# A two-layer decoder on one core: the first attention's scores from fp32r pairs in row tiles, wider query chunks, and PSUM in slots of two banks

## The chip, the cores and the metric

The kernel runs on one core of one Trainium2 chip. The metric is the device time of one execution in microseconds, from start to end on that core. TensorE multiplies matrices into PSUM (eight banks of 2 KiB per partition), VectorE and ScalarE read PSUM, GpSimd works on SBUF alone, and the DMA transfers are issued from the SyncE queue (SP).

## The reference

The input is `x`, 4 batches of 1024 tokens with 256 channels in fp32, and a context of 77 tokens a batch. Six blocks follow each other, each on a layer norm of `x` and added back to it: a causal attention with 16 heads of 16 dimensions and a linear bias by distance; a cross attention; a feed-forward block with quantized weights; then a second causal attention with squared scores and gates; a cross attention; and a feed-forward block with 4-bit quantization. The change is about the first of them:

```python
att = einsum('bhqd,bhkd->bhqk', q, k) / sqrt(16)
att = att + where(causal, slope[h] * (k_pos - q_pos), -inf)
y   = einsum('bhqk,bhkd->bhqd', softmax(att), v)
x   = x + y @ w_proj.T
```

and, through its use of PSUM, about the second attention too:

```python
P = where(causal, (q.k)**2 * exp(log_G[q] - log_G[k]), 0)   # scaled by its row's maximum
y = (P @ v) / sum(P)
```

## The kernel before, in words

The program is written as Python generators that are woven into each other by counts, and a scheduler of the framework then sets the final order on each engine when the program is built. That order is fixed at run time: each engine runs its instructions in it, and waits on semaphores.

The first attention of batch b (`A0`) runs together with a side stream: the preparation of weights for b = 0, and for later batches the cross attention and feed-forward block of batch b-1 (`XA`, `F0`). Towards the end of `A0` the front of the next batch (`qkv`, the first stacks, the first maxima) is woven in. Then comes the second attention (`A1`) with the blocks of the batch before as its side stream, and at the end the last feed-forward block in four lanes.

The first attention works in groups of four heads, 16 groups in all (4 batches of 4).

- `qkv` makes q and k transposed, splits each into three bf16 parts (L288 to L291, on ScalarE, VectorE and GpSimd) and stores them to DRAM (L294, L295). `stacks` loads them back as QS and KS, 96 rows in which the parts meet each other, and 12 to 14 rows more for the bias (L317 to L320). A product over these 108 or 110 rows gives a score near fp32.
- `a0_max` makes scores with queries on the partitions (tile M, L346), masks the diagonal with a matmul of the identity with a mask (L350), and takes row maxima on VectorE (L351). `a0_put_max` transposes the maxima and writes them as two more rows into QS (L377).
- `a0_main` makes the scores again with keys on the partitions (tile S, L392), in query chunks of 256, two heads to a bank. It masks (L394), ScalarE takes the exponential into P (L395), and after a lag of two units PV multiplies by V, which has a column of ones for the sum (L404). PV is plain fp32; its four heads go to four column tiles of 32.
- `o_out` transposes and divides (L418 to L425), `proj_res` projects and adds (L438 to L450).

PSUM tiles are one bank. `BANKS` gives each use its banks, taken in turn: in the first attention S has banks 0 and 1, M and Q banks 2 and 3, U bank 0; T and W of the side stream have 4, 5 and 6, and O has 7. In the second attention S, Q, U and D share 0 to 3. There, `scores` makes a unit of four heads in two banks (L867), takes absolute values of each bank on VectorE (L873) or ScalarE (L871), squares them (L875) and on the diagonal multiplies by a decay (L878); `decay` makes two banks with one exponential each (L841, L842).

Helpers record much under one line: L189 is every matmul of `mm3` (three fp32r products for one near fp32), and L177 and L178 are the split of an fp32 tile into a high and a low part.

Of the kernel before, what the change touches and what calls it, by code (L numbers as in the profile page):

```python
# [24 lines left out]
H = 16  # L25
D = 16
NEG = -30000.0
ABS_ACT = (1, 5)


def const_arrays():
# [6 lines left out]
    c["maskb"] = np.where(k > q, NEG, 0.0).astype(bf)  # L38
    c["maskTb"] = np.ascontiguousarray(c["maskb"].T)
# [22 lines left out]
    parts = []  # L62
    r = sl.astype(np.float64)
    for _ in range(3):
        p = r.astype(bf)
        parts.append(p)
        r = r - p.astype(np.float64)
    pos = np.arange(T)
    hi = (pos // 8 * 8).astype(np.float64)
    lo = (pos % 8).astype(np.float64)  # L70
    rq = np.zeros((H, 12, T), np.float64)
    rk = np.zeros((H, 14, T), np.float64)
    for h in range(H):
        r = 0
        for p in parts:
            s = float(p[h])
            for w in (hi, lo):
                rq[h, r], rk[h, r] = s, w
                rq[h, r + 1], rk[h, r + 1] = w, -s
                r += 2  # L80
        rk[h, 12:] = 1.0
    c["alq"] = np.ascontiguousarray(rq.transpose(1, 0, 2)).astype(bf)
    c["alk"] = np.ascontiguousarray(rk.transpose(1, 0, 2)).astype(bf)
# [3 lines left out]
NF0, NP0, NS0 = 10, 8, 30  # L87
# [3 lines left out]
class Kern:  # L91
    MAGIC = 12582912.0
    LAG0, LAG1 = 2, 2
    GQ, NQ = (2, 2, 2, 2), (12, 12, 12, 12)
    NW = ((25, 25, 38, 38),) * 4

    def const(self, *names):
        for nm, dt in names:
            t = self.cp.tile([96 if nm == "ind" else 128, 128], dt, name=nm)
            self.nc.sync.dma_start(t, self.c[nm])  # L100
            setattr(self, nm, t)
# [3 lines left out]
    def __init__(self, ctx, tc, ins, out, consts, nb=B):  # L105
# [23 lines left out]
    BANKS = (  # L129
        {"S": (0, 1), "M": (2, 3), "M0": (0, 1, 2, 3), "Q": (2, 3), "U": (0,), "D": (0, 1), "O": (7,), "T": (4, 5, 6), "W": (4, 5, 6)},  # L130
        {"S": (0, 1, 2, 3), "Q": (0, 1, 2, 3), "U": (0, 1, 2, 3), "D": (0, 1, 2, 3), "O": (7,), "T": (4, 5, 6), "W": (4, 5, 6), "TB": (0, 1, 2, 3), "WB": (0, 1, 2, 3)},
    )
# [19 lines left out]

    def p(self, tag):
        self.n += 1
        banks = self.BANKS[self.phase][tag]
        self.turn[banks] = self.turn.get(banks, -1) + 1
        k = banks[self.turn[banks] % len(banks)]
        return self.ps.tile([128, 512], F32, tag=f"B{k}", name=f"{tag}_{self.n}", bufs=1)
# [68 lines left out]
    def xT(self, xn, h, l, tag="T"):  # L227

        n = xn.shape[1]
        for c in range(2):  # L230
            ps = self.p(tag)
            for j in range(n):
                self.nc.tensor.transpose(ps[:, j * 128 : (j + 1) * 128], xn[:, j, c * 128 : (c + 1) * 128], self.ident)
            self.evac_hl(h[:, c, :], l[:, c, :], ps[:, : n * 128])
# [27 lines left out]
    def qkv(self, src, wd, nw, gl=None, w=None):  # L262
# [4 lines left out]
        for c in range(2):  # L267
            self.n += 1
            dr.append(self.dr.tile([8, 128, T], BF, tag=f"dr{c}", name=f"dr{c}_{self.n}", bufs=2))
        for half in range(2):  # L270
# [10 lines left out]
            for c in range(2):  # L281
                pt = self.t([128, 6, 512], BF, "qp")
                for s in range(2):
                    ps = self.p("Q")
                    o = s * 256 + c * 128
                    self.mm3(ps, [(wh[:, k, o : o + 128], wl[:, k, o : o + 128]) for k in range(2)], [(h[:, k, :], l[:, k, :]) for k in range(2)])
                    r = self.t([128, 512], F32, "qr")
                    nc.scalar.activation(pt[:, 5 * s], ps, AF.Copy)  # L288
                    nc.vector.tensor_tensor(r, ps, pt[:, 5 * s], ALU.subtract)
                    nc.gpsimd.tensor_scalar(pt[:, 1 + 3 * s], r, 1.0, 1.0, ALU.mult, ALU.mult)  # L290
                    nc.gpsimd.tensor_tensor(pt[:, 2 + s], r, pt[:, 1 + 3 * s], ALU.subtract)  # L291
                    yield
                d = dr[c]
                nc.sync.dma_start(d[1:7, :, hs].rearrange("t p n -> p t n"), pt)  # L294
                nc.sync.dma_start(d[0::7, :, hs].rearrange("t p n -> p t n"), pt[:, 0::5])  # L295
            n = 256 if gl is None else 272
            for e in range(4):
                ps = self.p("Q")
                i = half * 4 + e
                tk = slice(e * 128, (e + 1) * 128)  # L300
                self.mm3(ps[:, :n], [(h[:, k, tk], l[:, k, tk]) for k in range(2)], [(wh[:, k, 512 : 512 + n], wl[:, k, 512 : 512 + n]) for k in range(2)])
                nc.scalar.activation(vv[half][:, e, :, 0:16], ps[:, :256].rearrange("p (h e) -> p h e", h=H), AF.Copy)
                if gl is not None:
                    nc.scalar.activation(gl[:, i, :], ps[:, 256:272], AF.Copy)
# [3 lines left out]
    def stacks(self, g, dr, alibi):  # L308

        nc = self.nc  # L310
        QS = self.t([110, 4, T], BF, "QS")
        KS = self.t([110, 4, T], BF, "KS")
# [5 lines left out]
        if alibi:  # L318
            nc.sync.dma_start(QS[96:108], self.c["alq"][:, g * 4 : g * 4 + 4, :])
            nc.sync.dma_start(KS[96:110], self.c["alk"][:, g * 4 : g * 4 + 4, :])  # L320
# [3 lines left out]
    def prep_a0(self):  # L324
        self.wa0 = self.prep_w(self.i["L0_attn_w_attn"], 768, "wa0", 256)
        self.const(("identb", BF), ("maskb", BF), ("maskTb", BF))
# [6 lines left out]
    def a0_max(self, st, mt, tag="M"):  # L333
# [4 lines left out]
        def unit(pieces, diag, out):  # L338

            S = self.p(tag)  # L340
            n = len(pieces)
            w = pieces[0][3] - pieces[0][2]
            st_ = 512 // n
            Sv = S.rearrange("p (n k) -> p n k", n=n)
            for x, (hh, i, k0, k1) in enumerate(pieces):
                nc.tensor.matmul(Sv[:, x, 0:w], QS[:108, hh, i * 128 : (i + 1) * 128], KS[:108, hh, k0:k1], start=x == 0, stop=not diag and x == n - 1)  # L346
            if diag:
                r = self.maskb if n == 1 else self.maskb.unsqueeze(1).to_broadcast([128, n, 128])
                o = Sv[:, 0, w - 128 : w] if n == 1 else Sv[:, :, w - 128 : w]
                nc.tensor.matmul(o, self.identb, r, start=False, stop=True)  # L350
            nc.vector.tensor_reduce(out, Sv[:, :, 0:w], AX.X, ALU.max)  # L351

        for part in range(2):
            b0 = part * 4
            yield unit([(hh, b0, part * 512, part * 512 + 128) for hh in range(4)], True, mt[:, :, b0])
            for p in range(2):
                yield unit([(p * 2 + e, b0 + 1, part * 512, part * 512 + 256) for e in range(2)], True, mt[:, p * 2 : p * 2 + 2, b0 + 1])
            for i in (2, 3):
                for hh in range(4):
                    yield unit([(hh, b0 + i, part * 512, part * 512 + (i + 1) * 128)], True, mt[:, hh, b0 + i : b0 + i + 1])  # L360
        for i in range(4, 8):
            for hh in range(4):
# [906 lines left out]
```

## Time and profile before

| what | value |
|---|---|
| median of 3 runs | 2571.21 us (2570.82 to 2571.67) |
| profiled execution | 2593.41 us, its span 2591.4 us, granted TensorE clock 0.914 |
| TensorE matmul busy | 2214.7 us |
| VectorE busy | 1769.4 us |
| ScalarE busy | 1592.7 us |
| GpSimd busy | 1227.5 us |
| DMA, mean | 96 GB/s |
| first S to last S of the first attention (L392) | 137.6 to 1354.2 us |
| first S to last S of the second attention (L867) | 1371.9 to 2438.0 us |

A row of a group of instructions has the line, the engine and the operation, the tile written and those read, the shapes, the count, the busy time with the mean of one in ns, and the engine's idle time before them with what ended it. For matmuls the shape has rows and columns of the array in front ("110*128"). A plain fp32 matmul leaves two records in the trace, so L404 counts 2560 where the program has 1280. A row of a stretch has for each engine its busy time and count, then the granted TensorE clock, the DMA share and GB/s. A row of the timeline has the start in us, the time until the last of its instructions ends, and how many are merged. A row of waits has the total, the number of times, and the longest.

### The profile page before, as it was taken

To read this page: it belongs to the slowest core of one execution; us is meant where nothing else is said; L and a number is where in the kernel's file an instruction comes from. 1 tells how busy PE (TensorE), PEld (TensorE's weight loads), DVE (VectorE), ACT (ScalarE), POOL (GpSimd) and SP (SyncE) were. 2 spreads that over 40 slices of the span, in tenths; PEclk is the share of its full clock that TensorE was granted. 3 is DMA by queue.
4 is the path that set the end of the run, shared out by engine and by line. 5 is a ranking of instruction groups with operands and counts; after the bars stand their busy time and mean duration, and the time that the engine had idled before them with its cause. 6 is when DMAs were issued, how large, how long until landed. Compare 5 with 4: busy or idle time off the path is not lost.

```text
span 2591.4 us, 51361 instructions
## 1 busy us (share of the span) xinstructions
PE 2214.7 (85%) x19057; PEld 1575.9 (61%) x19094; DVE 1769.4 (68%) x3865; ACT 1592.7 (61%) x4099; POOL 1227.5 (47%) x2026
## 2 busy tenths in 40 slices
PE   5698889988989999899887997798879887879887
PEld 4455446754556755566545774476667666757676
DVE  3556555667566577566777677678857886677787
ACT  3255435666656676556666996786658674867532
POOL 6121302144321242213446467657875677565665
PEclk9689889999999999999997998898989998979888
DMA  8856540223652225122262211521162215333000
GB/s 228 184 133 178 163 103 13 68 62 108 158 146 58 67 81 183 41 68 55 73 189 80 73 53 64 168 83 47 64 167 72 57 65 165 86 111 83 10 9 17
DMA packets 170287, 248.44 MB, mean 96 GB/s; under 512 B 13734, under 2 KB 146166, under 8 KB 161430
## 3 DMA queue, kind: packets, MB, share of 16 engines
q1 hardware_dynamic: 170038, 245.17, 34.9%
q8 instruction: 150, 2.46, 0.4%
q14 instruction: 99, 0.81, 0.1%
HBM read 162.65 MB, written 82.21 MB: 94 GB/s over the span
## 4 chain that ended last, share of the span: by engine, by line
PE 50%; DVE 17%; DMA 13%; POOL 7%; ACT 5%; issue 3%; SPq 1%; POOLq 0%; ACTq 0%; DVEq 0%
PE T L189 8%; PE W L189 7%; PE O L404 6%; PE Q L189 4%; PE M L346 4%; PE S L392 4%; PE O L895 4%; PE S L867 3%; DMA KS<-c_alk 2%; DVE P L873 2%; DMA MD<-R 2%; DVE s_mt L351 2%; DMA UD<-R 1%; DMA QS<-dr 1%; PE T L716 1%
## 5 line engine op out<-in xcount | busy, mean ns | idle before, releaser
L351 DVE TENSOR_REDUCE s_mt<-M 128x1 f32<-128x512 f32 (+3 forms) x608 | 386.4, 656 | 161.7 <-PE M L350 112.8
L395 ACT ACTIVATE P<-S 128x512 f32<-128x512 f32 (+1 forms) x640 | 342.0, 564 | 167.5 <-PE S L392 87.1
L875 ACT ACTIVATE P<-P,eps 128x1024 f32<-128x1024 f32 (+1 forms) x320 | 341.6, 1091 | 68.5 <-DVE P L873 66.0
L873 DVE TENSOR_REDUCE P<-S 128x512 f32<-128x512 f32 (+1 forms) x480 | 281.4, 609 | 62.9 <-PE S L867 55.5
L189 PE MATMUL T<-R,xX 128*128 128x308 f32 (+1 forms) x1328 | 303.6, 340 | 13.2 <-DMA R<-g1d 3.1
L346 PE MATMUL M<-KS,QS 108*128 108x512 bf16 (+3 forms) x768 | 229.5, 347 | 54.7 <-DVE s_mt L351 21.3
L616 POOL TENSOR_TENSOR E<-E,s_xsm 128x616 f32<-128x616 f32 x88 | 108.3, 1231 | 323.5 <-DVE s_xsm L614 209.3
L392 PE MATMUL S<-QS,KS 110*128 110x256 bf16 (+1 forms) x1280 | 232.0, 270 | 27.9 <-ACT P L395 14.3
L613 ACT ACTIVATE E<-T,s_xmx 128x77 f32<-128x77 f32 x704 | 223.9, 361 | 41.4 <-DVE s_xmx L610 35.5
L189 PEld LDWEIGHTS T<-R,xX 128*128 128x128 f32 x1328 | 221.3, 197 | 42.4 <-ACT E L613 8.7
L189 PE MATMUL W<-R,xph 128*128 128x256 f32 (+2 forms) x1192 | 241.2, 299 | 4.3 <-DVE xpl L178 3.3
L867 PE MATMUL S<-QS,KS 96*128 96x256 bf16 (+1 forms) x1280 | 213.3, 273 | 35.1 <-DVE P L873 24.8
L404 PE MATMUL O<-P,V 128*32 128x256 f32 (+1 forms) x2560 | 241.4, 376 | 0.0
L189 PEld LDWEIGHTS W<-R,xph 128*128 128x128 f32 (+2 forms) x1192 | 195.0, 200 | 17.0 <-DVE xpl L178 4.9
L878 POOL TENSOR_TENSOR P<-P,y 128x512 f32<-128x512 f32 x128 | 168.2, 1320 | 68.0 <-ACT P L875 40.5
L189 PE MATMUL W<-R,xpl 128*128 128x256 f32 (+2 forms) x596 | 178.4, 299 | 3.3 <-DVE xpl L178 3.2
L392 PEld LDWEIGHTS <-KS 110*128 110x128 bf16 x1280 | 105.2, 100 | 110.2 <-issue 54.2
L867 PEld LDWEIGHTS <-KS 96*128 96x128 bf16 x1280 | 104.1, 100 | 102.3 <-issue 73.4
L613 ACT ACTIVATION_READ_ACCUMULATOR E<-T,s_xmx 128x1 f32 x704 | 166.1, 242 | 0.0
L177 ACT ACTIVATE xph<-W 104x128 fp32r<-104x128 f32 (+1 forms) x228 | 102.4, 475 | 97.1 <-PE W L627 35.3
L895 PE MATMUL O<-P,VsJ 128*32 128x128 f32 x3584 | 157.0, 282 | 5.3 <-ACT P L875 3.5
L346 PEld LDWEIGHTS <-QS 108*128 108x128 bf16 x768 | 69.4, 102 | 131.7 <-issue 103.2
(357 smaller groups left out, 5493.3 us busy)
## 6 DMA issues: line engine op xcount, KB each, us to landing
QS<-dr SPq DMA_DIRECT2D x72, 384.0 KB
KS<-dr SPq DMA_DIRECT2D x72, 384.0 KB
dr<-qp SPq DMA_DIRECT2D x32, 768.0 KB
MD<-R SPq DMA_DIRECT2D x24, 616.0 KB
UD<-R SPq DMA_DIRECT2D x24, 616.0 KB
R<-MD SPq DMA_DIRECT2D x22, 616.0 KB
R<-UD SPq DMA_DIRECT2D x22, 512.0 KB
R<-g1d SPq DMA_DIRECT2D x6, 1408.0 KB
```

The source lines that it names most:

```text
L189: nc.tensor.matmul(out, x, y, start=first and n == 0, stop=last and n == len(seq) - 1)
L346: nc.tensor.matmul(Sv[:, x, 0:w], QS[:108, hh, i * 128 : (i + 1) * 128], KS[:108, hh, k0:k1], start=x == 0, stop=not diag and x == n - 1)
L351: nc.vector.tensor_reduce(out, Sv[:, :, 0:w], AX.X, ALU.max)
L392: nc.tensor.matmul(S[:, e, 0:w], st[1][:110, hh, j * 128 : (j + 1) * 128], st[0][:110, hh, q0 : q0 + w], start=e == 0, stop=not dg and e == 1)
L395: nc.scalar.activation(P[:, 2 * p : 2 * p + 2, 256 - w :], S[:, :, 0:w], AF.Exp)
L404: nc.tensor.matmul(O[0][hh * 32 : hh * 32 + 32, o + o0 : o + 256], V[j // 4][:, j % 4, h * 17 : h * 17 + 32], P[:, hh, o0:], start=c % 2 = ...
L613: nc.scalar.activation(E[:, n * 77 : (n + 1) * 77], Sv[:, k, :], AF.Exp, bias=mx[:, n : n + 1], accum_out=sm[:, n : n + 1])
L867: nc.tensor.matmul(S[:, e, 0:w], st[g][1][:96, hh, j * 128 : (j + 1) * 128], st[g][0][:96, hh, q0 : q0 + w], start=e == 0, stop=e == 1)
L873: nc.vector.tensor_reduce(Pv, S[:, :, 0:w].unsqueeze(3), AX.X, ALU.max, apply_absolute_value=True)
L875: nc.scalar.activation(Pw, Pw, AF.Square, bias=self.eps1)
L878: nc.gpsimd.tensor_tensor(Pd, Pd, Ds[g, c][:, j - 2 * c], ALU.mult)
L895: nc.tensor.matmul(Oc[r, o0 : o0 + 128], lhs, P[:, hh, c0 : c0 + 128], start=j == 2 * c and i == 2 * c, stop=fin and i == 2 * c + 1)
```

## The change

q and k are rounded to two 12-bit parts, held as fp32r (high and low, L177 and L178's split), so that a head needs 48 rows of parts and 4 to 6 rows of bias, 54 at most. Two heads then stand above each other in the 128 partitions, one from row 0, one from row 64, and their matmuls address the array as two row tiles of 64, each writing a bank of its own. The bias rows are rounded on the chip once and kept in DRAM. The masks become four matmuls for each diagonal pair, two row tiles by two halves of a 64-row identity.

Query chunks grow from 256 to 512, and P becomes one tile for each pair of heads. PSUM banks 0 to 3 become two slots, A and B, of two banks each, which S, M, Q, U, D, TB and WB take in turn in both attentions. Maxima, exponentials, absolute values and decays work over both banks in one instruction. The counts of the weaving are adapted to the smaller number of units, and the lag of PV goes from two units to one. `a0_put_max` writes its rows with four transfers, and a group's stacks come with 14.

```diff
-    BANKS = (
-        {"S": (0, 1), "M": (2, 3), "M0": (0, 1, 2, 3), "Q": (2, 3), "U": (0,), "D": (0, 1), "O": (7,), "T": (4, 5, 6), "W": (4, 5, 6)},
-        {"S": (0, 1, 2, 3), "Q": (0, 1, 2, 3), "U": (0, 1, 2, 3), "D": (0, 1, 2, 3), ...},
-    )
+    SLOTS = {**{r: ("A", "B") for r in ("S", "M", "Q", "U", "D", "TB", "WB")}, "O": (7,), "T": (4, 5, 6), "W": (4, 5, 6)}
+    def pp(self, tag):
+        slots = self.SLOTS[tag]
+        self.turn[slots] = self.turn.get(slots, -1) + 1
+        k = slots[self.turn[slots] % len(slots)]
+        return self.ps.tile([128, 1 if k in (4, 5, 6, 7) else 2, 512], F32, tag=f"B{k}", ...)
...
     # qkv, first attention
+                        pt = self.t([128, 2, 512], F32R, "qp")
+                        self.evac_hl(pt[:, 0], pt[:, 1], ps)
+                        nc.sync.dma_start(dr[c][s, :, :, hs].rearrange("t p n -> p t n"), pt.bitcast(F32))
...
+    def pair_stacks(self, g, dr):
+        QS = self.t([128, 2, T], F32R, "QS")
+        KS = self.t([128, 2, T], F32R, "KS")
+        for s, st in enumerate((QS, KS)):
+            v = dr[c][s].rearrange("t (d h) n -> (t d) h n", h=8)
+            for e in range(2):
+                r = 64 * e + 4
+                hv = v[:, o + e : o + e + 3 : 2, :]
+                nc.sync.dma_start(st[r + 16 * s : r + 16 * s + 32].bitcast(F32), hv)
+                d = r + 32 - 32 * s
+                nc.sync.dma_start(st[d : d + 16].bitcast(F32), hv[0:16])
+        # and three short transfers of bias rows for each e
...
+    def mask(self, S, m, cols):
+        for half, (a, b) in enumerate(cols):
+            for e in range(2):
+                r = slice(64 * e, 64 * e + 64)
+                self.nc.tensor.matmul(S[:, e, a:b], self.id64[r, half], m[r, half, a:b], start=False, stop=half == 1)
...
     # a0_max, one unit
+            S = self.pp("M")
+            for e, r in enumerate(rows):
+                nc.tensor.matmul(S[:, e, 0:w], QS[r, pr, i * 128 : (i + 1) * 128], KS[r, pr, k0:k1], start=True, stop=not diag)
+            nc.vector.tensor_reduce(mt[:, :, pr, slot], S[:, :, 0:w], AX.X, ALU.max)
...
     # a0_main
+            q0 = max(j * 128, c * 512)
+            w = (c + 1) * 512 - q0
+            for pr in range(2):
+                P = self.t([128, 2, 512], F32, "P")
+                S = self.pp("S")
+                for e in range(2):
+                    r = slice(64 * e, 64 * e + 54)
+                    nc.tensor.matmul(S[:, e, 0:w], KS[r, pr, j * 128 : (j + 1) * 128], QS[r, pr, q0 : q0 + w], start=True, stop=j < 4 * c)
+                if j >= 4 * c:
+                    self.mask(S, self.mkT64, ((0, 64), (0, 128)))
+                nc.scalar.activation(P[:, :, 512 - w :], S[:, :, 0:w], AF.Exp)
+                Ps.append(P)
...
+                nc.tensor.matmul(O[0][hh * 32 : hh * 32 + 32, o0:], V[...], Ps[hh // 2][:, hh % 2, o0:], start=j == 0, stop=j == 4 * c + 3)
...
     # A1, scores: four heads in one slot
+            S = self.pp("S").rearrange("p b (h k) -> p (b h) k", h=2)
+            if self.absn % 4 == 1:
+                nc.scalar.activation(Pv, S[:, :, 0:w], AF.Abs)
+            else:
+                nc.vector.tensor_reduce(Pv, S[:, :, 0:w].unsqueeze(3), AX.X, ALU.max, apply_absolute_value=True)
...
-        run_all(weave(seg, 196, side, n))
+        run_all(weave(seg, 162, side, n))
```

## The prediction, made before the changed kernel was run

> **What bounds the kernel now.** I read the page's busy shares first, then the same numbers by stretch, then the order of time on TensorE, then who waits. The change sits almost wholly in the first attention, which fills 140 to 1370 us.
>
> ```profile
> PE 2214.7 (85%) x19057; PEld 1575.9 (61%) x19094; DVE 1769.4 (68%) x3865; ACT 1592.7 (61%) x4099; POOL 1227.5 (47%) x2026
> ...
> 140.00:1370.00 1230.00, 1102.68 (x8575) 707.80 (x8600) 802.07 (x1736) 729.22 (x2054) 359.10 (x507) 0.94 0.38 102
> 1370.00:2440.00 1070.00, 905.73 (x9390) 695.54 (x9402) 781.25 (x1755) 774.30 (x1807) 714.38 (x1314) 0.91 0.31 87
> 2440.00:2592.00 152.00, 114.97 (x716) 105.59 (x708) 120.61 (x234) 46.10 (x148) 94.58 (x106) 0.87 0.03 11
> ```
>
> In the first-attention stretch TensorE is busy for 1103 of 1230 us (90%) at 0.94 of its clock, VectorE for 65%, ScalarE for 59%, the DMA engines for 38%. So this stretch is priced in TensorE time. But a busy TensorE is pipelined; what an instruction costs is the step from its start to the next start:
>
> ```profile
> 709.36 0.39 PE L346 MATMUL M<-KS,QS 108*128 108x512 bf16 x1
> 709.59 0.60 PE L392 MATMUL S<-QS,KS 110*128 110x256 bf16 x4
> 710.12 0.64 PE L404 MATMUL O<-P,V 128*32 128x256 f32 x8
> 710.69 0.39 PE L346 MATMUL M<-KS,QS 108*128 108x512 bf16 x1
> ...
> 742.35 0.63 PE L404 MATMUL O<-P,V 128*32 128x256 f32 x4
> 742.91 0.39 PE L392 MATMUL S<-QS,KS 110*128 110x256 bf16 x2
> 743.23 0.41 PE L404 MATMUL O<-P,V 128*32 128x128 f32 x4
> 743.57 0.38 PE L189 MATMUL Q<-WAh,yTl 128*128 128x256 f32 x1
> ```
>
> 512 bf16 columns of M take 0.23 us. A plain fp32 matmul leaves two records, so "O x8" is four heads and "O x4" two. Four heads of 256 columns take 0.57 us (710.12 to 710.69), but two heads take 0.56 (742.35 to 742.91): heads that follow each other run together in their column tiles of 32, and a run of two wastes half. 128 columns take 0.34 (743.23 to 743.57), so each further 128 cost about 0.21. Four S took 0.53, where four by 0.115 are 0.46: entering the column tiles costs some 0.09.
>
> ```profile
> L351 DVE TENSOR_REDUCE s_mt<-M 128x1 f32<-128x512 f32 (+3 forms) x608 | 386.4, 656 | 161.7 <-PE M L350 112.8
> L395 ACT ACTIVATE P<-S 128x512 f32<-128x512 f32 (+1 forms) x640 | 342.0, 564 | 167.5 <-PE S L392 87.1
> ...
> PE M L346 <- DVE s_mt L351: 20.4, 36, 3.5
> PE M L346 <- DMA KS<-c_alk: 19.8, 6, 5.2
> PE S L392 <- ACT P L395: 14.3, 17, 3.4
> PE S L392 <- DMA QS<-VsJ: 12.6, 3, 6.1
> ```
>
> The evictions wait more for TensorE (162 and 168 us) than TensorE waits for them (20 and 14 us).
>
> **The change part by part.** One group is four heads of one batch; there are 16. I take steps at full clock and divide the sum by 0.94.
>
> Before, a group costs: M, 18432 columns at 0.23 per 512, 8.3 us; S the same, 8.3; masks, 4096 columns for M, 1.8, and 16 of 0.115 for S, 1.8; PV, 20 units, 16 at 0.57 and 4 at 0.345, 10.5, times 1.25, because the built order has 400 runs of PV where 320 would do (238 of four heads, 124 of two), 13.1; entering a run, 25 by 0.09, 2.3. Sum 35.6.
>
> *QK in row tiles.* 48 pairs a group replace 128 matmuls. No row tile runs in this trace. If the two tiles run together, a pair of 512 takes 0.23: 11.0 us a group. If they run one after the other it is the columns: 17.5. The row says 128-column fp32 weights can be had every 0.12 us (fp32 matmuls of 256 columns step by 0.12 at 743.79), and a pair needs two loads, so narrow pairs are no cheaper than 0.23, and a lone pair has its second load ahead of its second matmul. The Trainium skill, "TensorE: Matmul & The Clock Gate", Part 3, has tiles of different row groups start about 4 ns apart; by that rule it is 11.0, by the row 0.30 a pair. I take 0.30: 14.4.
>
> *Masks.* 38 matmuls a group become 128 of 64 to 128 columns, each with a weight load. Alone, a 128-column bf16 matmul steps by 0.056 (an S pair of 128 at 742.02 needs 0.12): 7.2; two at a time 3.6. I take 5.4, against 3.6 before.
>
> *PV.* Each pair of heads now has a P tile of its own, and the built order no longer keeps four heads together: 374 runs of two, one of four, ten of one. A run of two costs 0.345 at 128 columns and 0.21 for each further 128: 0.985 at 512. Per group 12 by 0.985, 4 by 0.77, 4 by 0.56, 4 by 0.345: 18.5 us, plus 24 entries by 0.09, 2.2. Wider chunks save weight loads, but these hide already. This is +5.3 us a group, and it is read from a row of the same form.
>
> *Changes of tiling.* The order counts 801 changes between full array and column tiles before, and 771 involving column tiles after, plus 589 new ones between full array and row tiles. Into a PV run the trace shows 0.09, out of it 0.57-0.43 = 0.14 (0.43: four passes of 256 columns at 0.107 each). Whether row tiles pay the same, it can't show. The Trainium skill, "TensorEngine Tiling (Array Packing)", Key Properties, says that changing the mode drains the engine; 589 by 0.11 is 4.0 us a group by the rule, 0 without it. I take 2.5.
>
> Sum: 14.4+5.4+18.5+2.2+2.5 = 43.0, or +7.4 a group; 16 groups over 0.94: +126 us. Bounds: 11.0+3.6+18.5+2.2+0 = 35.3, that is -5 us; 17.5+7.2+18.5+2.2+4.0 = 49.4, +235 us. Some of it falls into the 127 us in which TensorE stands idle; I let three quarters through: **+95** (-5 to +235).
>
> *Slots of two banks.* S had two banks and M, Q two others; now S, M, Q and U take turns in A and B. An eviction over both banks takes 1.21 us on VectorE (L726's 1024-wide maximum) and 1.04 on ScalarE (L742), where a single bank came free after 0.68 and 0.61. Per instruction this saves: 29 us on VectorE, 30 on ScalarE over the stretch, off the path. But TensorE works in order, so S now waits for M's maximum and M for S's exponential, and everything behind it (PV, the side work's T and W) waits too. Along the built order, at the steps above, one turn of a slot in ten leaves 0.35 us between S's last matmul and the M that needs its slot. Shortfalls add to about 180 us, against 80 by the same sum before, where the trace shows 40 to 50 us. Halved: **+50** (0 to +110).
>
> *DMA.* A group's stacks are 14 issues on SP instead of 6, the maxima 4 instead of 2. SP spends 0.35 to 0.6 us on each (QS<-VsJ 0.55), so S at a group's start gets its maxima 1.2 us later and M its stacks 4 us later; TensorE already waits for them (12.6 and 19.8 us). Bytes are equal, packets larger. **+20** (0 to +60). Rounding alq and alk sends 0.66 MB in and out at the start, at 205 GB/s: **+6**. Dropping the GpSimd splits of q and k is worth nothing: POOL is 29% busy there.
>
> *Second attention and end.* One instruction over two banks saves 27 us of VectorE and about the same of ScalarE; TensorE's work stays. D, U and Q now hold whole slots, and the order leaves a median 1.5 us between two S in one slot, from 2.0, while the eviction grows from 0.68 to 1.21: **+5** (-25 to +35). In the last 150 us two of four lanes draw pairs from A and B: **+5** (0 to +12).
>
> Sum 95+50+20+6+5+5 = 181 us, against the profiled execution's 2593.4 us. That is 0.9% above the median of the runs shown, 2571.2; scaled, 2571+180 = 2750.
>
> **The rivals.** *Slower, as summed* (0.72): PV in runs of two plus the shared slots eat the row tiles' gain. *Row tiles one after the other, with drains* (0.13): TensorE +235 with little of it hidden, slots +60, the rest as above: about 2571+310 = 2880. For it: no row tile was ever seen here; against it: column tiles do run together. *Faster* (0.12): pairs run together without a drain, masks two at a time, TensorE at -5; the shorter evictions then cut 20 us of its waits, the second attention gains 25 us and DMA costs 6: about 2527. For it: VectorE and ScalarE lose 60 us of work; against it: it needs the best end of four prices at once. It decides at 35.6 us a group: with PV at 20.7, QK, masks and changes together must stay under 14.9. *No difference* (0.03).
>
> **How the numbers follow.** Time 2750, the first case's. The range, 2600 to 2890, takes in TensorE's low bound with a little waiting and most of the serial case. A difference of 0.2% is about what a measurement can tell. Faster 0.12, same 0.03, slower 0.85.
>
> **What would show it.** PV steps near 0.98 us for two heads of 512; two records of QK starting within 0.12 us or 0.2 apart; idle before M and S put down to ScalarE's exponential and VectorE's maximum; busy time of VectorE down by 55 us. I am wrong if PV's four heads run together, or if TensorE's idle time shrinks between 140 us and the end of the first attention.

## The result, and the profile after

The changed kernel takes 2929.0 us (median of 4 runs, 2907.7 to 2942.8), the kernel before 2571.4 us beside it. The ratio is 1.1376, with a 95% interval of 1.1297 to 1.1455: slower by 358 us. The direction was forecast, the size was not: 2929 lies above the range of 2600 to 2890.

All that follows is of the kernel after, whose profiled execution took 2937.2 us with a span of 2935.5: from its page the busy shares, the two evictions and PV; then the first attention as one stretch, beside the same row of the kernel before; then TensorE's waits in that stretch. In a row of a stretch the columns are the busy time of TensorE, its weight loads, VectorE, ScalarE and GpSimd, then the granted TensorE clock, DMA share and GB/s.

```profile
PE 2393.3 (82%) x18964; PEld 1599.3 (54%) x18998; DVE 1732.5 (59%) x3382; ACT 1571.3 (54%) x3634; POOL 1157.4 (39%) x1962
...
L409 DVE TENSOR_REDUCE s_mt<-M 128x2 f32<-128x1024 f32 (+3 forms) x384 | 364.5, 954 | 228.2 <-PE M L393 162.6
L450 ACT ACTIVATE P<-S 128x1024 f32<-128x1024 f32 (+3 forms) x384 | 301.7, 813 | 326.6 <-PE S L393 256.0
...
L459 PE MATMUL O<-P,V 128*32 128x512 f32 (+3 forms) x1536 | 362.1, 551 | 0.0
```

Before, then after:

```profile
137.00:1372.00 1235.00, 1107.68 (x8597) 711.56 (x8622) 805.87 (x1742) 732.50 (x2061) 361.57 (x509) 0.94 0.38 102
128.00:1683.00 1555.00, 1285.30 (x8502) 723.70 (x8526) 809.51 (x1559) 716.77 (x1788) 323.71 (x469) 0.87 0.31 84
```

```profile
PE S L447 <- DMA QS<-ot: 70.0, 10, 11.6
PE M L406 <- ACT P L450: 37.5, 52, 3.3
PE S L447 <- DVE s_mt L409: 23.9, 26, 2.8
PE M L426 <- DVE s_m L425: 14.6, 8, 4.7
```

Read against before: every engine but TensorE has less work than it had, and the first attention alone, 137 to 1372 us before, now fills 128 to 1683. TensorE's busy time in it rose from 1108 to 1285 us, but its idle time also rose, from 127 to 270 us, and its clock fell from 0.94 to 0.87. All three parts matter. The waits name new pairs: M waits for ScalarE's exponential of S, and S for VectorE's maximum of M, as two uses of one slot do. Above them stands the maxima's way into QS by DMA (from the tile ot, which holds them once they are transposed).

The same sum from the starts of TensorE's matmuls (from the first S of the first attention to the first S of the second; a gap over 150 ns counts as idle, and work in the spans of half clock counts half, the other half being "loss"):

| kernel | stretch | idle | work at full clock | loss to half clock |
|---|---|---|---|---|
| before | 1234 | 123 | 1049 | 62 |
| after | 1555 | 267 | 1145 | 144 |

So 321 us more are 144 of idle, 96 of work and 82 of clock. The second attention took 22 us more (1066 to 1088), the end 10 us more, and the start 10 us less; that makes the difference of the spans, 344 us.

### The profile page after: what moved, and what is told of

It reads as the page before. It is cut to its first block, busy times and chain, and to the rows that moved or that the text cites. A ratio compares the mean times of both kernels' runs of the same rounds, so it can differ in the third digit from the quotient of the medians.

```text
span 2935.5 us, 50432 instructions
## 1 busy us (share of the span) xinstructions
PE 2393.3 (82%) x18964; PEld 1599.3 (54%) x18998; DVE 1732.5 (59%) x3382; ACT 1571.3 (54%) x3634; POOL 1157.4 (39%) x1962
## 4 chain that ended last, share of the span: by engine, by line
PE 53%; DVE 16%; DMA 11%; ACT 7%; POOL 6%; issue 4%; SPq 1%; ACTq 0%; DVEq 0%; POOLq 0%
PE O L459 9%; PE T L202 9%; PE W L202 7%; PE Q L202 5%; PE M L406 4%; PE S L447 3%; PE O L952 3%; DVE P L930 3%; PE S L924 3%; DMA UD<-R 2%; DMA KS<-dq 2%; DMA QS<-ot 2%; ACT P L450 2%; ACT P L932 1%; DVE s_mt L409 1%
## 5 line engine op out<-in xcount | busy, mean ns | idle before, releaser
L409 DVE TENSOR_REDUCE s_mt<-M 128x2 f32<-128x1024 f32 (+3 forms) x384 | 364.5, 954 | 228.2 <-PE M L393 162.6
L450 ACT ACTIVATE P<-S 128x1024 f32<-128x1024 f32 (+3 forms) x384 | 301.7, 813 | 326.6 <-PE S L393 256.0
L459 PE MATMUL O<-P,V 128*32 128x512 f32 (+3 forms) x1536 | 362.1, 551 | 0.0
L930 DVE TENSOR_REDUCE P<-S 128x1024 f32<-128x1024 f32 (+1 forms) x240 | 255.5, 1074 | 90.1 <-PE S L924 83.1
L447 PE MATMUL S<-QS,KS 54*128 54x512 f32 (+3 forms) x768 | 183.2, 461 | 135.1 <-DMA QS<-ot 70.0
L924 PE MATMUL S<-QS,KS 96*128 96x256 bf16 (+1 forms) x1280 | 186.6, 275 | 67.8 <-DVE P L930 38.7
L447 PEld LDWEIGHTS S<-QS,KS 54*128 54x128 f32 x768 | 82.3, 199 | 259.0 <-issue 94.3
L406 PE MATMUL M<-KS,QS 52*128 52x512 f32 (+3 forms) x768 | 182.3, 472 | 50.0 <-ACT P L450 37.5
L406 PEld LDWEIGHTS M<-KS,QS 52*128 52x128 f32 x768 | 78.5, 201 | 183.2 <-ACT P L450 75.6
L782 POOL TENSOR_TENSOR R<-wst 128x256 f32<-128x256 f32 x128 | 93.5, 743 | 186.6 <-DVE wst L781 172.7
```

Source lines behind the costliest of these rows:

```text
L406: nc.tensor.matmul(S[:, e, 0:w], QS[r, pr, i * 128 : (i + 1) * 128], KS[r, pr, k0:k1], start=True, stop=not diag)
L409: nc.vector.tensor_reduce(mt[:, :, pr, slot], S[:, :, 0:w], AX.X, ALU.max)
L447: nc.tensor.matmul(S[:, e, 0:w], KS[r, pr, j * 128 : (j + 1) * 128], QS[r, pr, q0 : q0 + w], start=True, stop=j < 4 * c)
L450: nc.scalar.activation(P[:, :, 512 - w :], S[:, :, 0:w], AF.Exp)
L459: nc.tensor.matmul(O[0][hh * 32 : hh * 32 + 32, o0:], V[j // 4][:, j % 4, h * 17 : h * 17 + 32], Ps[hh // 2][:, hh % 2, o0:], start=j == 0 ...
L924: nc.tensor.matmul(S[:, hh, 0:w], st[g][1][:96, hh, j * 128 : (j + 1) * 128], st[g][0][:96, hh, q0 : q0 + w], start=hh % 2 == 0, stop=hh % ...
```

## The experiments

Ratios are to the kernel before in the same job, whose median was 2571 to 2588 us; so kernels are compared by their ratios, and a difference of ratios is told in us as its product with 2571. The last four columns are as above.

| kernel | median | ratio (95%) | stretch | idle | work | loss |
|---|---|---|---|---|---|---|
| after | 2929.0 | 1.1376 (1.1297 to 1.1455) | 1555 | 267 | 1145 | 144 |
| E1 PV in runs of four | 2875.6 | 1.1124 (1.1091 to 1.1157) | 1473 | 275 | 987 | 210 |
| E2 maxima earlier | 2900.2 | 1.1219 (1.1193 to 1.1246) | 1502 | 218 | 1136 | 148 |
| E3 both | 2845.8 | 1.1021 (1.0981 to 1.1060) | 1457 | 250 | 980 | 227 |
| E4 after, short maxima | 2903.6 | 1.1238 (1.1208 to 1.1268) | 1515 | 235 | 1140 | 140 |
| E6 after, whole array | 2864.1 | 1.1079 (1.1052 to 1.1107) | 1472 | 235 | 1162 | 75 |
| E7 E1, whole array | 2748.0 | 1.0630 (1.0594 to 1.0666) | 1373 | 285 | 1005 | 83 |
| E8 E3, whole array | 2726.7 | 1.0553 (1.0522 to 1.0584) | 1332 | 238 | 1004 | 90 |
| E9 E8's order of work in one-bank slots | 2574.4 | 0.9996 (0.9980 to 1.0011) | 1219 | 138 | 1023 | 58 |
| E10 E8, short maxima | 2634.6 | 1.0221 (1.0185 to 1.0256) | 1263 | 204 | 998 | 62 |
| E12 E9, maxima later | 2585.1 | 1.0045 (1.0029 to 1.0061) | 1228 | 149 | 1025 | 54 |

### E1 to E4: the order of PV, the end of the maxima, the length of an eviction

```diff
 # E1, pv: the heads of the pair that is ready last come first, and each stays behind the one before it
-            for hh in range(4):
+            for hh in (2, 3, 0, 1):
                 h = g * 4 + hh
-                nc.tensor.matmul(O[0][hh * 32 ...
+                mm = nc.tensor.matmul(O[0][hh * 32 ...
+                if hh != 2:
+                    self.tc.keep_in_program_order(mm)
 # E2: the next group's maxima end at two thirds of the group
-    NW = ((24, 24, 36, 26),) * 4
+    NW = ((36, 36, 48, 26),) * 4
 # E4: the maximum of every fourth column
-            nc.vector.tensor_reduce(mt[:, :, pr, slot], S[:, :, 0:w], AX.X, ALU.max)
+            nc.vector.tensor_reduce(mt[:, :, pr, slot], S[:, :, 0:w:4], AX.X, ALU.max)
```

E1:

> The changed kernel with one edit: the four PV matmuls of a unit are issued in the order of heads 2, 3, 0, 1 and pinned behind each other, so that in the built order 187 of 193 runs of PV have four heads (374 of 385 had two), and changes of tiling fall from 1360 to 1062. Theory (PV in runs of two costs TensorE its column tiles' concurrency): PV falls from 18.5 to about 9.4 us a group and 300 changes at 0.11 go, some 170 us at full clock, all on the path: 2745 us (2700 to 2790), with less time at half clock as well. Rival (the stretch is bound by waits on shared slots and on the maxima, and TensorE's time only fills them): a gain under 60 us, TensorE's idle time in the first attention growing from 266 us by what PV saves.

E2:

> The changed kernel with one edit: the weaving counts of the maxima go from 24 to 36 for each 12 units of the main work (48 in the third group), so that a group's maxima end after two thirds of the group before and not with it. Theory (S at a group's start waits for four transfers of maxima, 101 us in 16 waits on TensorE and its weight loads): these waits go, and the time at half clock after them: 2929 falls to 2840 (2800 to 2880). Rival (the wait only changes place, because more maxima crowd the two slots in the first two thirds): within 25 us of 2929, waits of S for VectorE's maximum and of M for ScalarE's exponential growing by as much.

E3, the edits of E1 and E2 together:

> Both edits of the two kernels before. If they act on different things, the gains add: about 2660 us (2600 to 2720). If both only trade one wait for another, it stays over 2800.

E4:

> The changed kernel, but the row maximum reads every fourth column only, so the maxima are not the true ones; all other work stays. VectorE holds a slot for about 0.4 us instead of 1.21 and loses some 240 us of work. Theory (slots shared by S and M stall TensorE, which works in order): waits of S for VectorE's maximum go, M's for ScalarE stay: 40 to 80 us faster. Rival (the slots are not what stalls it): within 20 us of 2929.

Measured: E1 gained 65 us, E2 40, both together 91, E4 35, each give or take the 20 us of the interval of the kernel after. The theories had expected 184, 89, 269, and 40 to 80; so all three edits help and the first two nearly add up, but each brings less than its theory said, and none is the main cause.

E1 is the odd one. Its work at full clock fell by 158 us, yet the stretch fell by 82: the loss to half clock grew from 144 to 210 us. A part of E1's trace that stays at half clock, as one row and then a piece of it in order of time:

```profile
843.80:891.60 47.80, 39.85 (x211) 19.16 (x211) 22.97 (x32) 14.46 (x21) 0.58 (x4) 0.50 0.36 89
```

```profile
851.48 1.22 PE L447 MATMUL S<-QS,KS 54*128 54x512 f32 x4
853.40 1.50 PE L406 MATMUL M<-KS,QS 52*128 52x512 f32 x4 [0.69 <-ACT P L450]
854.69 0.38 PE L393 MATMUL M<-mk,id 64*128 64x128 bf16 x4
855.00 1.93 PE L459 MATMUL O<-P,V 128*32 128x512 f32 x8
856.87 0.79 PE L406 MATMUL M<-KS,QS 52*128 52x512 f32 x2
857.46 0.62 PE L447 MATMUL S<-QS,KS 54*128 54x512 f32 x2
858.99 0.80 PE L447 MATMUL S<-QS,KS 54*128 54x512 f32 x2 [0.90 <-DVE s_mt L409]
```

For 47.8 us the clock is 0.50 (the number before the DMA share), with TensorE busy for 39.9. PV now runs in fours ("O x8"), but takes 1.87 us for 512 columns (855.00 to 856.87). Either the short waits in brackets hold the half clock, or the work itself does: E5 to E8 tell these apart.

### E5: kinds of work alone

Matmuls without any wait inside, in eight blocks, each behind some 18 us in which TensorE stands idle, so that each begins at half clock. No attention is computed.

```diff
+        for n in range(64):                     # block 2: row pairs with their masks
+            pair((S, M)[n % 2], r, 54, stop=False)
+            masks((S, M)[n % 2], h)
...
+        for n in range(60):                     # block 5: row pairs and whole-array passes in turn
+            pair((S, M)[n % 2], r, 54)
+            nc.tensor.matmul(F, r[:, 0:128], r[:, 512:1024], start=True, stop=True)
```

> A kernel of its own, with none of the decoder's work: eight blocks of matmuls back to back, each after some 15 us in which TensorE waits. Blocks: 96 fp32r matmuls of 512 columns over the full array; 96 row-tile pairs of 54 rows and 512 columns; 64 such pairs with four masks each; 32 PV runs of four heads by 512; 20 times two masked pairs and a PV run (the changed kernel's mix); 60 times a pair and a full-array matmul in turn; 96 bf16 matmuls over 110 rows; 20 times four of these and a PV run (the mix of before). Theory H (row tiles do not count as enough work to release the half clock): the full-array blocks leave half clock within 7 us, the row-tile blocks and the changed mix stay at half, however dense they are. Rival (only small waits between them hold the half clock): every block leaves it within 7 us, since none waits inside. Changes of tiling: 0.1 us each way in the alternating block if they drain, a pair then 0.23 alone and 0.43 in turn; else no more than 0.23 each.

Measured: blocks 1, 2 and 5 as stretches, and then a piece of block 5 in order of time.

```profile
65.30:90.00 24.70, 24.64 (x192) 21.31 (x192) 0.00 (x0) 1.06 (x1) 0.00 (x0) 0.89 0.00 1
109.00:155.30 46.30, 46.21 (x384) 26.21 (x384) 0.00 (x0) 1.10 (x2) 0.00 (x0) 0.50 0.00 1
278.80:365.70 86.90, 86.84 (x180) 34.28 (x180) 0.02 (x1) 1.00 (x1) 0.00 (x0) 0.50 0.00 0
```

```profile
320.00 0.79 PE L94 MATMUL F<-r 128*128 128x512 f32 x1
320.72 0.79 PE L51 MATMUL M<-r 54*128 54x512 f32 x2
321.45 0.79 PE L94 MATMUL F<-r 128*128 128x512 f32 x1
```

Row pairs alone (65 us) leave the half clock after 5.5 us and have 0.89 over the block. Single pairs with their masks (109 us) stay at 0.50 for all of 46 us, pairs and whole-array passes in turn (279 us) for all of 87 us. TensorE is "busy" for 46.21 of 46.30 and 86.84 of 86.90 us: no wait holds the clock there. The other five blocks (whole array in fp32r, bf16 over 110 rows, PV, both attention mixes) have 0.88 or more over the block. So neither expectation holds as it stands: row tiles alone do release the half clock, and short waits are not needed to keep it. The two mixes prove less than they seem to, because both blocks began with six or more PV matmuls in a row. The timeline shows a clue: a step is 0.72 us whichever kind it is, where row pairs alone, still at half clock, start 0.43 us apart (66.34, 66.77). Every change between row tiles and the whole array thus costs 0.30 us.

The masked pairs lose time too, and there the tiling does not change: pairs and masks both use row tiles of 64. A piece of block 2:

```profile
149.32 0.77 PE L51 MATMUL S<-r 54*128 54x512 f32 x2
149.90 0.38 PE L57 MATMUL S<-h 64*128 64x64 bf16 x4
150.04 0.77 PE L51 MATMUL M<-r 54*128 54x512 f32 x2
```

Here a pair takes 0.58 us to the next start, 0.15 more than alone. A step of a pair and its masks is 0.72 us, and its columns (512, 64 and 128) would stream in 0.59, an estimate from 0.43 for 512.

### E6 to E8: the same kernels on the whole array

The row tiles are undone, with all that they bring along: q and k are in three bf16 parts over 108 and 110 rows, as before, their stacks come with the transfers of before, and the masks use the 128-row identity. Chunks of 512, P in pairs, the lag and the slots of two banks stay. A cut from the difference to the kernel after:

```diff
-            for e, r in enumerate(rows):
-                nc.tensor.matmul(S[:, e, 0:w], QS[r, pr, i * 128 : (i + 1) * 128], KS[r, pr, k0:k1], ...)
+            for e in range(2):
+                nc.tensor.matmul(S[:, e, 0:w], QS[:108, 2 * pr + e, i * 128 : (i + 1) * 128], KS[:108, 2 * pr + e, k0:k1], ...)
```

E6, after without row tiles:

> The changed kernel without its row tiles: q and k again in three bf16 parts over 110 rows of the full array and one mask a head, as before; kept are the chunks of 512, P in pairs, the slots of two banks and one instruction over both. Theory H (row tiles hold the half clock): TensorE's full-clock work is nearly the same as the changed kernel's (QK +3 us a group, changes of tiling 775 instead of 1360, so -4), but the half clock falls to the 0.94 of before: 2929 becomes about 2830 (2780 to 2870). Rival (waits on slots and maxima cause the half clock): clock and time stay within 40 us of 2929.

E7, with PV in runs of four:

> The same without row tiles, and PV's four heads pinned together (188 runs of four). Theory H: now PV's gain of some 150 us at full clock shows up, unlike the 53 us that it brought with row tiles: about 2670 us (2610 to 2730). Rival (slots bind): no better than 2876, the kernel with row tiles and PV pinned, by more than 50 us.

E8, with the maxima earlier as well:

> The same again with the maxima ending after two thirds of the group before. If the waits for the maxima are on the path, 30 to 60 us faster than without; this is the version nearest to the kernel before, and if two-bank slots and chunks of 512 are worth anything it comes under 2580. If the slots are the cost, it stays over 2620.

Measured: E6's 2848 us (its ratio times 2571) lies in the range of its theory, E7's 2733 3 us above; E8's earlier maxima are worth 20 us, not 30 to 60, and it stays over 2620. The three pairs of kernels differ by the row tiles and what they bring along (fp32r parts, half-identity masks, more transfers). Without these the times are 76, 127 and 120 us shorter (after to E6, E1 to E7, E3 to E8). The table says by what: TensorE's work at full clock *rises* by 17, 18 and 24 us, so the row tiles did save work; the loss to half clock falls by 69, 127 and 137 us; idle moves by -32, +10 and -12. And runs of four in PV are worth 115 us on the whole array (E6 to E7), against 65 with row tiles. The clock took back what the row tiles, and better packing beside them, saved. The data type alone is not what keeps it down: the whole-array block of E5 is fp32r as well and came back. The first attention as one stretch, of E3 and then of E8:

```profile
128.00:1585.00 1457.00, 1202.03 (x8530) 739.82 (x8531) 804.37 (x1561) 712.91 (x1788) 326.73 (x470) 0.81 0.33 90
```

```profile
135.00:1467.00 1332.00, 1088.19 (x7530) 689.90 (x7529) 798.57 (x1560) 710.95 (x1784) 363.81 (x520) 0.92 0.36 96
```

0.81 against 0.92 of the clock. E8 is still 5.5% above the kernel before, though its work is 45 us less. Its idle time is 115 us more.

### E9 and E10: slots of one bank, and shorter maxima

E10 is E8 with E4's edit. E9 takes the kernel before and gives it the chunks of 512, P in pairs, a lag of one, PV in fours and maxima that end at two thirds. Slots, evictions and maxima stay one bank wide, in both attentions. So against E8 it differs by the slots, by the width of every eviction, by the pieces in which the maxima are made, and by the counts of the weaving that go with them. A cut from the difference to E8:

```diff
             for pr in range(2):
                 P = self.t([128, 2, 512], F32, "P")
-                S = self.pp("S")
                 for e in range(2):
+                    S = self.p("S")
                     nc.tensor.matmul(S[:, 0:w], KS[:110, 2 * pr + e, ...], QS[:110, 2 * pr + e, q0 : q0 + w], ...)
...
+                    nc.scalar.activation(P[:, e, 512 - w :], S[:, 0:w], AF.Exp)
-                nc.scalar.activation(P[:, :, 512 - w :], S[:, :, 0:w], AF.Exp)
```

> The kernel before with one part of the change alone: query chunks of 512 with the P tiles in pairs and a lag of one, PV in runs of four heads, the maxima finished at two thirds of the group. Everything else is the kernel before's: bf16 stacks of 110 rows over the whole array, slots of one bank, one exponential and one maximum per bank, no row tiles. It differs from the whole-array variant with both edits (2727 us) by the slots of two banks and by the shape of the maxima. Theory 'slots': what that variant still has over the kernel before (140 us, of them 115 us of TensorE idle in the first attention) is the wait of a slot of two banks for its evacuation; with single banks the idle time of the first attention falls from 238 us to below 160, and with 46 us less of full-clock work than in the kernel before the time is 2500 to 2590. Theory 'chunk': the idle comes from the longer steps and the lag of one, which this kernel keeps: it stays at 2650 to 2730.

> The whole-array variant with both edits (2727 us), and the maximum is taken over every fourth column only, so that VectorE's reduction of 1024 columns takes about 0.4 us instead of 1.2 (the maxima are then not the rows' own). If the slots wait for VectorE: about 100 us faster (S and M waiting for the maximum were 39 us in the profile, what is queued behind them more). If they wait for ScalarE's exponential or for the DMA: at most 30 us faster, as with the row tiles (25).

Measured: E9 is level with the kernel before (0.9996), 143 us below E8, within the range of its theory 'slots'; E10 is 85 us below E8, near the 100 expected if the slots wait for VectorE. TensorE's waits in the first attention, E8 first, then E9:

```profile
PE M L376 <- DMA KS<-c_alk: 43.8, 9, 5.4
PE M L376 <- ACT P L418: 32.9, 60, 2.2
PE S L415 <- DVE s_mt L379: 24.6, 44, 2.0
PE S L415 <- ACT P L418: 12.1, 15, 4.0
PE M L376 <- DVE s_mt L379: 11.4, 15, 1.3
```

```profile
PE M L346 <- DMA KS<-c_alk: 26.1, 6, 5.6
PE S L391 <- ACT P L394: 18.6, 30, 3.5
PE S L391 <- DMA QS<-VsJ: 16.7, 5, 5.8
PE M L346 <- DVE s_mt L351: 10.5, 29, 1.7
```

In E8 the two largest slot waits are crossed: M waits for the exponential, S for the maximum, 57.5 us and 104 times. In E9 M and S have banks of their own, and only the straight waits are left, 29 us. Idle time in the stretch fell by 100 us, more than these lines; the rest sits in other waits, as the one for KS (43.8 to 26.1). That it comes from what is queued behind a waiting S or M, and is then late for its own partners, is argued, not shown. The second attention points the same way. It took 1071 to 1105 us in the traces of the nine decoder kernels with two-bank slots, and 1042 to 1066 in the three with one-bank slots (before, E9, E12), some 35 us less in the mean. E10 says that the width of the eviction counts in it: VectorE's maximum alone shortened, work hardly changed (1004 to 998), idle fell by 34 us, loss to half clock by 28, the rest outside the stretch. In E4, with row tiles and slow PV, the same edit gave 35 us. In the kernel that it started from, S and M waited 25 us for the maximum (23.9 and 1.0), in E8 36 (24.6 and 11.4); whether that is the reason wasn't tested.

E9 also prices the rest of the change: larger chunks, P in pairs, the lag of one and PV in fours save 26 us of TensorE work and cost 15 us of idle; in the time they are worth nothing that can be told from zero.

### E11: how much change of tiling the clock bears

> Eight blocks of matmuls alone without any wait inside, each behind about 18 us in which TensorE idles, so that each begins at half clock: row pairs of 54 rows and full-array passes of 512 columns in turn, in runs of 1, 2, 4 and 8; the same in runs of 1 with 64 rows; four column tiles and one full pass in turn; two row pairs and then their masks; one row pair and two column tiles in turn. (No attention is computed.) In the first such kernel row pairs alone, column tiles alone, full passes alone and two masked pairs beside four column tiles came back to full clock within 6 us, but pairs and full passes in turn (87 us) and masked pairs (46 us) never did. Theory 'drain': TensorE counts the drain at a change of tiling as idle; the block in runs of 1 stays at half clock whether 54 or 64 rows are used, runs of 4 and 8 come back, runs of 2 may do either; the step of a change is the same per change in all runs, about 0.15 us at full clock. Theory 'row tiles': work on row tiles itself does not count; runs of 8 stay at half clock too. Theory 'rows': 64 of 64 rows comes back where 54 does not. Column tiles and full passes in turn: the drain theory says half clock if their change drains as long (0.15 us against steps of 0.25 and 1.0), else full.

```diff
+        for k, n in enumerate((1, 2, 4, 8)):    # blocks 0 to 3
+            for m in range(48 // n):
+                for x in range(n):
+                    pair((S, M)[x % 2], r, 54)
+                for x in range(n):
+                    full(r)             # the whole-array pass of E5's block 5
```

Measured: blocks 0, 1, 2, 3 last 69.5, 55.3, 28.9 and 26.3 us for the same 96 row matmuls and 48 whole passes. A piece of block 1 (runs of two), two pieces of block 2 (runs of four), and block 6, two pairs and then their masks, as a stretch:

```profile
111.94 1.22 PE L60 MATMUL F<-r 128*128 128x512 f32 x2
113.09 0.79 PE L51 MATMUL S<-r 54*128 54x512 f32 x2
113.69 0.63 PE L51 MATMUL M<-r 54*128 54x512 f32 x2
114.25 1.22 PE L60 MATMUL F<-r 128*128 128x512 f32 x2
```

```profile
187.20 2.02 PE L60 MATMUL F<-r 128*128 128x512 f32 x4
189.15 0.50 PE L51 MATMUL S<-r 54*128 54x512 f32 x2
...
209.50 0.50 PE L51 MATMUL S<-r 54*128 54x512 f32 x2
...
210.65 1.20 PE L60 MATMUL F<-r 128*128 128x512 f32 x4
211.78 0.51 PE L51 MATMUL S<-r 54*128 54x512 f32 x2
```

```profile
425.96:451.27 25.31, 25.31 (x384) 15.34 (x384) 0.00 (x0) 1.03 (x1) 0.00 (x0) 0.89 0.01 2
```

The record of the clock begins only at 189 us in this trace, so blocks 0 and 1 are read by their steps. Runs of two repeat after 2.31 us (111.94 to 114.25): four passes at 0.43 leave 0.60 for two changes, 0.30 each, the half-clock price of E5, and it is the same at the block's end, so it never left half clock. Runs of one step by 0.72, the same price, and a block of runs of one with 64 instead of 54 rows takes 69.5 us at a recorded clock of 0.50: the unused rows are not the reason. Runs of four and eight come back to full clock. There a period of four is 2.28 us (209.50 to 211.78), eight passes at 0.23 and two changes of 0.2.

So work on row tiles does release the clock when it is long enough between changes. At half clock a change takes 0.30 of every 0.72 us in runs of one (41%) and 26% in runs of two, and neither came back. Runs of four began at 185.19 us and were at full clock by 189.15, before their first two runs were over: of these 3.96 us the eight passes fill 3.44, so some 13% was lost. Masked pairs fit. Single pairs with masks lose 18% of their step of 0.72 us and stay; in twos (block 6) two pairs and their masks take 1.31 us at half clock (427.31 to 428.62) where 1.18 would stream, 10% lost, and they come back. There the first pair behind masks takes 0.57 us and the second 0.43, so the loss comes with the step from bf16 masks to an fp32r pair; what it is, the runs don't show. One rule fits all these blocks: time lost between matmuls, which the profile shows as busy, counts for the clock like idle time, and the half clock stays where the lost share is above a bound between some 13 and 18%. What the clock gate really counts, the runs don't show. The theories 'row tiles' and 'rows' are refuted. The two blocks with column tiles also ended at full clock, but they began with four or more PV matmuls in a row, so they don't test coming back from half clock in turns.

That such losses, at changes of tiling or between masks and pairs, held the clock in the attention itself is argued from this and from E6 to E8, not isolated there: an order of the attention with fewer changes but the same row tiles wasn't tried. Nor were row tiles in slots of one bank, where each head's bank comes free by itself.

### E12: can E9 be made faster than before?

> The kernel with one-bank slots and chunks of 512 (2574 us, level with the kernel before), with its maxima finished at some 85 instead of 67 hundredths of the group, the only change. In its trace TensorE waited 26 us for the next group's KS stack (6 times) in the maxima, which start early, and 17 us for the maximum's rows in QS (5 times). If the early start is what is late: the first wait falls below 15 us and the time by 5 to 20 us, which would make it faster than both kernels. If the late end decides: the wait for the rows in QS grows by as much and the time stays within 10 us or rises by up to 20.

```diff
-    NW = ((57, 57, 66, 38),) * 4
+    NW = ((44, 44, 60, 38),) * 4
```

Measured: 1.0045, 13 us slower than E9. The wait for KS did not fall (26.1 to 28.6 us), nor did the one for the rows in QS grow (16.7 to 16.9); S's own wait for the exponential grew from 18.6 to 23.3. Neither account of the expectation holds in its mechanism. No version here beats the kernel before.

## Why the prediction was right or wrong, point by point

**PV in runs of two: right.** The steps after, at full clock, are 0.98 us for two heads of 512 columns (164.49 to 165.48), 0.77 for 384 (below, 701.35 to 702.12), 0.56 for 256 and 0.34 for 128, as forecast:

```profile
701.35 0.84 PE L459 MATMUL O<-P,V 128*32 128x384 f32 x4
702.12 0.39 PE L406 MATMUL M<-KS,QS 52*128 52x256 f32 x2
```

Undoing it (E1) removed 158 us of full-clock work from the stretch.

**QK in row tiles: close, for another reason.** The two tiles start 3 or 4 ns apart, so they run together, and the rival with serial tiles is refuted, although its 2880 is nearest to the result. A piece of the kernel after in order of time:

```profile
713.42 0.33 PE L447 MATMUL S<-QS,KS 54*128 54x128 f32 x2
713.58 0.26 PE L393 MATMUL S<-mkT,id 64*128 64x64 bf16 x4
713.78 1.04 PE L775 MATMUL T<-R,xX 128*128 128x512 bf16 x4
714.75 0.33 PE L447 MATMUL S<-QS,KS 54*128 54x128 f32 x2
714.91 0.26 PE L393 MATMUL S<-mkT,id 64*128 64x64 bf16 x4
714.98 0.47 PE L406 MATMUL M<-KS,QS 52*128 52x512 f32 x2
715.30 0.26 PE L393 MATMUL M<-mk,id 64*128 64x128 bf16 x4
```

A pair of 128 columns takes 0.16 us, one of 512 takes 0.32, so narrow pairs are cheaper than the 0.23 I set as a floor and wide ones dearer; the weight loads don't limit. The mean over the pairs of a group, from start to start at full clock, is 0.30, as I took it, but it has the losses at changes in it that I added once more; that the two agree is luck. Four masks take 0.07 us when a row tile follows (714.91 to 714.98) and 0.20 when the whole array does (713.58 to 713.78). The difference of 0.13 fits the drain that the rule of the Trainium skill ("TensorEngine Tiling (Array Packing)", Key Properties) announced; weighing it at something over half was right in kind. Of the two rules weighed for a pair, the 4 ns of the Trainium skill, "TensorE: Matmul & The Clock Gate", Part 3, agrees with the trace here, and E5's pairs alone step by 0.23 us at full clock. Two smaller readings were off: the columns of the serial case come to 16.6 us a group at 0.23 for 512, not 17.5, and entering the column tiles shows 0.07 us, not 0.09.

**The sum of TensorE's work: right within a fifth.** Forecast 16 groups by 7.4 us, 118 us at full clock; measured 96. That is in part two errors that cancel. PV was priced at 85 of the 118 and the row tiles with their masks and changes at 34. E6, which has the PV of after on the whole array, has 113 us more work than the kernel before, and the row tiles then took 17 away (E6 to after).

**"I ... divide the sum by 0.94": wrong, 74 us.** Dividing by before's clock turned 118 us into 126, 8 us for the clock. The loss to half clock rose by 82 us, and 69 of these go when the row tiles are undone (E6). I priced a change of tiling once, as 0.11 us of time, and not a second time, as activity; E5 and E11 show that it can keep the clock down, though in the attention itself that stays argued.

**"I let three quarters through" and the slots, +50: wrong, about 105 us.** A quarter of the work was to vanish in TensorE's idle time (-31 us), and slots and DMA were to add 50 and 20: together +39 us of idle. Measured +144. Three terms. The slots: one-bank slots and evictions instead of two-bank ones take 100 us of idle out of the stretch (E8 to E9), twice the 50 and near its bound of 110. In the prediction's words one turn of a slot in ten was short by little; I halved the shortfall because the trace before showed half of it. But before, M and S had separate banks, and M waited for the maximum and S for the exponential; now each waits for both. The maxima's way by DMA: 70 us of waits after, against 12.6 before. The number of transfers is not it, since E6 with two instead of four waits 65.7 us; the maxima end at the end of the group, and where they end earlier (E2) this wait is gone. A wait of M for KS of 61.8 us stands in its place, and idle falls by 49 us and the time by 40. The third: the idle time that was to hide a quarter of the work hid nothing that the sums show.

**Second attention +5, end +5, start +6:** +22, +10 and -10. The first is within its bound of +35. That kernels with one-bank slots are faster there than all with two-bank slots fits the slots as its reason.

**VectorE down by 55 us:** 37 us (1769.4 to 1732.5). Neither sign of being wrong came: PV's four heads did not run together, and TensorE's idle time grew.

## What to carry to other kernels

Price a change of tiling twice, as time and as clock: here TensorE stayed at half speed without one idle gap where row tiles and the whole array took turns, and came back where the runs were four long. Two uses that share PSUM slots are tied to each other's evictions: the wider evictions saved VectorE and ScalarE some 60 us of work (37 and 21), and the kernel with them (E8) took 143 us longer than the one without (E9). And work taken from the busiest engine does not all reach the end time: from E6 to E7 157 us less of it brought 50 us more idle.

## What the runs showed of the hardware that I had not expected

The granted clock of 0.50 held for 86.9 us in which TensorE was busy for 86.84 (E5), and for 69.5 us in E11. The Trainium skill, "TensorE: Matmul & The Clock Gate", Part 1, has full clock follow a window of about 3.4 us of sustained work; in these blocks it didn't, in the others it did within some 6 us. "Busy" in a profile is then not what the gate counts: with 18% or more of the time lost between matmuls there was no return, with some 13% there was. The recorded spans of the clock in E5 and E11 last 17.07, 20.48, 23.89, 27.31 us and so on, whole multiples of 3.41 us but for those that the trace's end cuts off; so here the clock changed only at such steps. A change between row tiles and the whole array cost 0.30 us at half clock and 0.2 at full. In the attention this showed as a clock of 0.81 (E3) where the same order of work without row tiles had 0.92 (E8).
